# Order of VectorE and SyncE work around the attention steps of a four-layer kernel

## The chip, the cores and the metric

The kernel runs on one core of a Trainium2 chip. TensorE (PE) multiplies matrices, VectorE (DVE), ScalarE (ACT) and GpSimd (POOL) compute beside it, SyncE (SP) issues most of the transfers, and GpSimd issues the gathers. The metric is the time of one execution on the device in microseconds. The kernel before has a median of 1561.31 us in 4 runs (1559.86 to 1563.71).

## The reference

An input x of 8 sequences, 128 tokens each and 512 features, all in 32-bit floats, goes through four layers of the form x + ffn(cond(x)):

```
x = x + L0_ffn(L0_cond(x))   # gated MLP with adapters; two experts of 8
x = x + L1_ffn(L1_cond(x))   # low-rank adapters chosen by sequence; 8 weighted experts
x = x + L2_ffn(L2_cond(x))   # attention over cached and new keys; linear layer with a routed low-rank part
x = x + L3_ffn(L3_cond(x))   # linear layer, two of 8 experts; 16 of 64 rank-8 experts
```

The change lies in the third layer's attention. It has 32 query heads and 8 key heads of width 128. The queries and keys of the 128 new tokens are normalised (root mean square), scaled and rotated by position. Each sequence attends to 512 cached tokens, gathered through a table of pages, of which those behind the sequence's length are masked, and to its own 128 new tokens:

```
scores = einsum('bqhd,bkhd->bhqk', q, k_all) * SCALE
probs = softmax(where(valid, scores, -1e30))
o = einsum('bhqk,bkhd->bqhd', probs, v_all)
out = einsum('bse,de->bsd', o.reshape(b, s, 4096), Wo)
```

## The kernel before, in words

All of it is one program with x held on chip. Attention takes 32 steps, n = 0 to 31: eight key heads (`qd`), and for each of them four pairs of sequences (`p`). A key head serves four query heads, so a step treats two sequences j = 0, 1 with four heads each. The steps are software-pipelined; the body of the loop in `run` (L1271) does, in this order:

- `weigh(n, 0)` (L1118): five score matmuls of sequence 0 (`st`, keys by queries, four chunks `kT` of cached keys and one `kTn` of new keys), each followed by ScalarE's exponential into `pT`.
- `added(n, 0)` (L1140): four VectorE sums over the chunks, into `part`: chunks 0 and 1, chunks 2 and 3, the two together, chunk 4. It is a generator, so a step can be taken out of it and the rest later.
- `divided(n - 1)` (L1183): the output of the step before times the inverse sums `R`, into `oT`; `outputs(n - 1)` (L1189): four VectorE sums (`os`) of blocks of `oT`.
- `project(n + 1)` (L996): queries, keys and values of the next step. The product is done by a scheme with seven block products in place of eight (`seven`, L948), with sums of input blocks (`xs` by `tokens`, weight `factors`) made by VectorE beforehand. `rotate` (L1037) then makes the crossed terms of the rotation on GpSimd (`vq`, `vk`) and the straight terms on VectorE; that of the keys is handed back as a function, `keys_terms`.
- `leave(n - 1)` (L1197): the product with Wo, again by `seven` (`wo_one`, `wo_two`, `wo_six`), added to `y`. At named places in it `seven` calls hooks, and these decide where VectorE's other work stands.
- `fetch(n + 1)` (L1109), `gather`: reading of the turned queries and keys, gathers of values.
- `weigh(n, 1)` mixed with `mix(n, 0)` (`av`, L1172), `added(n, 1)`, `summed(n)` (L1149, sum over keys by matmuls with ones, `sum`), `inverted(n)` (L1160, the reciprocal, copied four times by VectorE and spread over partitions by three SP transfers `R<-R`), `mix(n, 1)`, then the cached keys and token sums of step n + 2.

Queries and keys are turned by a VectorE transpose of 32 by 32 blocks into a tile `qkt` or `kt`. Both are the same one buffer. SP writes the tile to device memory in four transfers (`turned_new`, `turned_cached`) and reads it back in another layout (`qT`, `kTn`, `kT`). So the next transpose into that buffer waits until the writes before it have landed.

In `seven` the hook "u2" stands right after VectorE's two sums `u`. Then come two matmuls into the bank `six`, VectorE's addition of that bank into y (`c22`), and the hook "c22". The bank's last matmuls multiply by the fourth weight factor, and they write the bank that VectorE has to read first:

```
into(p5, s1, t1, fresh)
kept(dve.tensor_tensor(u[:, 1], p6, u[:, 0], ALU.add))
now("u1")
kept(dve.tensor_tensor(u[:, 2], p5, u[:, 1], ALU.add))
now("u2")
into(six, s3, t3, True)
c22(six, u[:, 2])
now("c22")
into(one, a12, b21, False)
...
into(six, a22, t4, False)
```

The Wo weights of a key head are loaded behind its first pair; of their four factors (`o_s`) one to three are made in `project` of the following step, and the last one in `leave` of that step, so in steps 1, 5, 9 and so on to 29. Step 0 has no output of a step before it, and step 31 no next one to project; for both, `run` has branches of their own.

What is wrapped in `kept` stays in the program's order on its engine. What is not, is placed by the scheduler that builds the program. The two weight loads of the fourth part of the kernel, `load_w2` and `load_aw` (L1742, L1746, 1 MB each, called in step 30), and the addition of a bias to x on GpSimd (`shifted`, L1779) are not wrapped. The profile shows them where the scheduler put them: the loads in step 30, the two halves of the bias in steps 28 and 30.

After step 31 follow the linear layer of layer three and layer four.

Of the kernel before, what the change touches and what calls it, by code (L numbers as in the profile page):

```python
# [783 lines left out]
def attention(tc, a, x, ident, lens, kvrow, part, ww, wop, ypool, sums, rot, eps, psa, c2, chunks, mm):  # L784
# [7 lines left out]
    pe, act, dve, pool, sp = nc.tensor, nc.scalar, nc.vector, nc.gpsimd, nc.sync  # L792
# [52 lines left out]
    W, WO = {}, {}  # L845
# [45 lines left out]
    def every(ops):  # L891
        for _ in ops:
            pass
# [34 lines left out]
    def tokens(n, tag="xs"):  # L928


        qd, p = steps[n]
        b = 2 * p
        if 0 < qd < NQ - 1 and p in kept_sums:
            S[n]["A"] = kept_sums[p]
            return iter(())
        parts = [x[:, 2 * h : 2 * h + 2, (b + j) * P : (b + j + 1) * P] for j in range(2) for h in range(2)]
        if 0 < qd < NQ - 1:
            if not kept_sums:
                late.append(late[0].tile([P, NP, 4, 2, P], F32, tag="yT", name="xs_all"))
            S[n]["A"], ops = combine(late[1][:, p], *parts)  # L940
            kept_sums[p] = S[n]["A"]
        else:
            S[n]["A"], ops = combine(
                wk.tile([P, 4, 2, P], F32, tag=tag, name=f"xs_{n}", **({"bufs": 1} if tag == "xs" else {})), *parts
            )
        return ops
# [118 lines left out]
    def rotated(n):  # L1065
        for m in "qk":
            r, u = S[n]["r" + m]
            kept(dve.tensor_tensor(r, r, u, ALU.add))
# [6 lines left out]
    def normed(n):  # L1075

        s = S[n]
        r, rs = s["rq"][0], s["rs"]
        kept(dve.reciprocal(rs, rs))
        kept(dve.tensor_tensor(r, r, rs[:, :, 0:REP].unsqueeze(3).to_broadcast([P, 2, REP, HD]), ALU.mult))  # L1080

    def turn_cached(n):

        s = S[n]
        t = wk.tile([P, 4, 8, 32], F32, tag="kt", name=f"kt_{n}", bufs=1)
        for j in range(2):
            kept(dve.transpose(
                t[:, :, 4 * j : 4 * j + 4, :], s["kc"][j].rearrange("p c (b d) -> p b c d", b=4)
            ))
        s["kT"] = wk.tile([P, 4, 8, 32], F32, tag="kT", name=f"kT_{n}")  # L1090
        written(turned[n], t)
        return lambda: kept(sp.dma_start(s["kT"], turned[n].rearrange("b i a m d -> (b i) a m d")))
# [5 lines left out]
    def turn(n, by=(sp,)):  # L1098

        s = S[n]  # L1100
        m = 2 * REP
        t = wk.tile([P, 4, m + 2, 32], F32, tag="kt", name=f"qkt_{n}", bufs=1)
        done = kept(dve.transpose(t, s["both"].rearrange("p m (b d) -> p b m d", b=4)))
        s["qT"] = wk.tile([P, 4, m, 32], F32, tag="qT", name=f"qT_{n}", bufs=1)
        s["kn"] = wk.tile([P, 2, 4, 32], F32, tag="kTn", name=f"kTn_{n}", bufs=1)
        written(turned_new[n], t, by)
        return done

    def fetch(n, between=lambda: None):  # L1109
        s = S[n]  # L1110
        m = 2 * REP
        src = turned_new[n].rearrange("b i a m d -> (b i) a m d")
        kept(sp.dma_start(s["qT"], src[:, :, 0:m, :]))
        between()
        for j in range(2):
            kept(sp.dma_start(s["kn"][:, j], src[:, :, m + j, :]))
# [72 lines left out]
    def outputs(n):  # L1189
        oT = S[n]["oT"]  # L1190
        S[n]["oA"], ops = combine(
            late[0].tile([P, 4, 2, P], F32, tag="os", name=f"os_{n}"),
            *(oT[:, j, 2 * h : 2 * h + 2, :] for j in range(2) for h in range(2)),
        )
        return ops
# [75 lines left out]
    def run(pool_, end_of, bank, keep):  # L1271
        late.append(pool_)
        y2 = ypool.tile([P, NB, D], F32, tag="y", name="y2")
        Y.append(y2)
        pool.memset(y2, 0.0)

        idle = psa.tile([P, 512], F32, tag="mm", name="idle_q", bufs=3)
        for _ in range(3):
            kept(pe.matmul(idle, x[:, 0, 0:P], x[:, 0, 0:512], start=True, stop=True))
        for j in range(2):  # L1280
            squares(1, "q", j, range(REP))
            squares(1, "k", j, (0,))
        rotate(1)()
        gather(1, "v")
        roots(1)
        rotated(1)
        normed(1)
        turn(1)
        end, prepared = None, iter(())
        w_ops, wo_ops = iter(()), WO[0].factors()  # L1290

        def some(ops, k=1):
            return lambda: [next(ops, None) for _ in range(k)]

        for n, (qd, p) in enumerate(steps):

            after = n + 1 if 0 < n < len(steps) - 1 else None
            weigh(n, 0)
            sums_of, outs = added(n, 0), iter(())
            next(sums_of)  # L1300
            some(w_ops)()
            if n:
                divided(n - 1)
                outs = outputs(n - 1)
            every(sums_of)
            if after:
                project(after, {
                    "u2": lambda: (every(outs), every(w_ops), some(wo_ops)()),
                    "c22": lambda: (turn_cached(2)() if n == 1 else None, some(wo_ops, 2)()),
                    "c11": lambda: (squares(after, "k", 0, (0,)), squares(after, "q", 0, (0, 1))),  # L1310
                    "c12": lambda: squares(after, "q", 0, (2, 3)),
                })
                keys_terms = rotate(after)
                if n + 2 < len(steps):
                    if steps[n + 2][1] == 0:
                        weights(steps[n + 2][0])
                    gather(n + 2, "k")
                leave(n - 1, {
                    "one": lambda: (
                        squares(after, "q", 1, range(REP)), squares(after, "k", 1, (0,)), roots(after),  # L1320
                    ),
                    "u2": lambda: (keys_terms(), every(wo_ops)),
                    "c22": lambda: (rotated(after), normed(after), turn(after)),
                })
                fetch(after)
                gather(after, "v")
            elif n:
                every(outs)
                leave(n - 1)
            else:  # L1330
                read_cached = turn_cached(1)
                every(tokens(2))
                gather(2, "k")
            if n + 2 == len(steps):
                end.load_w2()
                end.load_aw()
                end.shifted()
            mixed = mix(n, 0)
            weigh(n, 1, {2: (some(mixed),), 3: (some(mixed),), 4: (some(mixed, NC),)})
            if n == 0:  # L1340
                fetch(1, read_cached)
            every(added(n, 1))
            if 0 < n < len(steps) - 2 and steps[n + 2][1] == 0:
                w_ops = W[steps[n + 2][0]].factors()
                some(w_ops, 2)()
            summed(n)
            inverted(n)
            if n == 5:
                prepared = end.prepare(bank, lambda shape, name: wk.tile(shape, F32, tag="xs", name=name, bufs=1))
            next(prepared, None)  # L1350
            every(mix(n, 1))
            next(prepared, None)
            if n and p == 0:
                out_weights(qd)
                wo_ops = WO[qd].factors()
            if 0 < n < len(steps) - 2:
                turn_cached(n + 2)()
                every(tokens(n + 2))
            if n == 3:
                kept(keep())  # L1360
            if n == 4:
                end = end_of(kept)

            if qd == NQ - 1 and p:
                for j in range(2):
                    end.turn(y2, 2 * (p - 1) + j, bank)
            if n + 2 == len(steps):
                end.low(0, bank)
                end.anchors(0, bank)
        divided(n)  # L1370
        every(outputs(n))
        end.product(0, "st", bank)
        leave(n)
        return y2, end

    return SimpleNamespace(begin=begin, first=first, run=run, scratch=scratch)


# [307 lines left out]
def ending(tc, a, out, x, ident, bias3, experts, early, tile_of_w2, tile_of_aw, chunks, mm, kept=lambda i: i):  # L1686
# [4 lines left out]
    pe, act, dve, pool, sp = nc.tensor, nc.scalar, nc.vector, nc.gpsimd, nc.sync  # L1691
# [48 lines left out]
    W = {}  # L1740

    def load_w2():  # L1742
        W["2"] = tile_of_w2([P, DC, D], "WT2")
        sp.dma_start(W["2"], chunks(a["W2T"]))

    def load_aw():  # L1746
        W["a"] = tile_of_aw([P, DC, D], "AwT")
        sp.dma_start(W["a"], chunks(a["AwT"]))

    def turn(y2, b, bank):  # L1750
        if not Y2T:
# [387 lines left out]
```

## Time and profile before

| | us |
|---|---|
| median of 4 runs | 1561.31 |
| range of the runs | 1559.86 to 1563.71 |
| the profiled execution | 1558.25 |
| its span, first to last instruction | 1556.4 |
| TensorE busy in the span | 1521.5 |
| VectorE busy | 1023.6 |
| GpSimd busy | 828.8 |
| layers one and two, up to the first steps of attention | 330 |
| attention, steps 0 to 31 (330.61 to about 1402) | 1072 |
| the rest of layer three | 32 |
| layer four | 122 |

How to read what follows. A row of the timeline has the start in us from the span's start, the length, the engine, the line of the kernel, the operation, out<-in by the program's names, the shape and the count; in brackets stands the idle time of the engine ahead of it and what ended that. A 32-bit matmul instruction of the program shows as two, so `x4` are two of them. An instruction's listed length includes the time in which its result drains, so rows of one engine can overlap. The table of waits gives for each pair of waiting and releasing line the total in us, how often, and the longest. In the table by stretches, PEclk is the share of TensorE's clock that was granted. "Landing" is the time at which a transfer's last completion is recorded.

### The profile page before, as it was taken

The numbers are of one execution on the slowest core, as the hardware profiler recorded it, in microseconds if no ns is written. First come the engines' busy times: TensorE is split into PE (matmuls) and PEld (weight loads), VectorE is DVE, ScalarE is ACT, GpSimd is POOL, SyncE is SP. The second block draws the span as 40 slices with busy tenths as digits, with TensorE's granted clock in tenths as the row PEclk, the third lists the DMA queues.
The fourth block names the chain that finished last, engine by engine and source line by source line (L and its number), as shares of the span: only waits on it lengthen the run. The fifth ranks groups of instructions, "written<-read, shape, count | busy, mean of one in ns | idle before, by whom it ended". The sixth has DMA issues, their size and how long they took to land.

```text
span 1556.4 us, 18566 instructions
## 1 busy us (share of the span) xinstructions
PE 1521.5 (98%) x5991; PEld 930.3 (60%) x5991; DVE 1023.6 (66%) x1963; ACT 538.3 (35%) x1324; POOL 828.8 (53%) x842
## 2 busy tenths in 40 slices
PE   9999999989999999999999999999999999999998
PEld 7888886435555555556555556555555555568743
DVE  4665334477878777777877778777777878743141
ACT  1111110143445443445444445444445434321110
POOL 1341105285767777767777667777667777600000
PEclk9999999999999999999999999999999999999899
DMA  9111002143654444553454444455444435530000
GB/s 301 43 42 31 1 0 65 48 131 106 173 157 141 143 123 126 151 156 99 132 164 131 140 121 136 113 147 169 131 126 141 121 102 152 150 87 12 0 21 36
DMA packets 156682, 169.89 MB, mean 109 GB/s; under 512 B 54144, under 2 KB 127040, under 8 KB 156448
## 3 DMA queue, kind: packets, MB, share of 16 engines
q1 hardware_dynamic: 138144, 131.27, 29.7%
q0 software_dynamic: 17056, 36.49, 7.8%
q10 hardware_dynamic: 1376, 0.85, 0.2%
q8 instruction: 50, 0.82, 0.2%
q14 instruction: 56, 0.46, 0.1%
HBM read 113.89 MB, written 42.07 MB: 100 GB/s over the span
## 4 chain that ended last, share of the span: by engine, by line
PE 89%; DVE 5%; DMA 2%; POOL 1%; issue 1%; ACT 1%; SPq 0%; DVEq 0%; ACTq 0%; POOLq 0%
PE av L1177 17%; PE st L1126 16%; PE g L362 8%; PE q_six L962 7%; PE q_one L962 5%; PE q_five L962 5%; PE wo_two L962 5%; PE dn L362 5%; PE wo_six L962 3%; PE wo_one L962 3%; PE eo_l L53 3%; PE z L53 2%; PE h L1704 2%; PE o L53 2%; PE midp_l L53 1%; PE sum L1155 1%
## 5 line engine op out<-in xcount | busy, mean ns | idle before, releaser
L905 POOL DMA_INDIRECT kn<-in_k_cache,kvrow_k x256 | 281.4, 1099 | 73.3 <-issue 66.0
L1177 PE MATMUL av<-pT,vals 128*128 128x512 f32 x640 | 300.1, 599 | 0.0
L905 POOL DMA_INDIRECT vals<-in_v_cache,kvrow_v x256 | 260.3, 1017 | 73.4 <-issue 42.5
L1130 ACT ACTIVATE pT<-st,hide 128x512 f32<-128x512 f32 x256 | 176.0, 688 | 328.1 <-PE st L1126 328.1
L1126 PE MATMUL st<-qT,kT 128*128 128x512 f32 x512 | 235.8, 593 | 3.0 <-DMA qT<-turned_new 3.0
L1051 POOL TENSOR_TENSOR vq<-q,txq 128x256 f32<-128x256 f32 x128 | 118.3, 954 | 172.6 <-ACT sqq L1035 116.9
L1177 PEld LDWEIGHTS av<-pT,vals 128*128 128x128 f32 x640 | 119.5, 191 | 144.9 <-issue 142.8
L1126 PEld LDWEIGHTS st<-qT,kT 128*128 128x128 f32 x512 | 96.9, 190 | 111.5 <-issue 106.7
L1146 DVE TENSOR_TENSOR part<-pT 128x512 f32<-128x512 f32 x128 | 88.4, 693 | 79.2 <-ACT pT L1130 79.0
L962 PE MATMUL q_one<-q,x 128*128 128x384 f32 x256 | 93.0, 486 | 0.0
L1035 ACT ACTIVATE sqq<-q 128x128 f32<-128x128 f32 x256 | 79.4, 310 | 11.6 <-DVE q L1011 4.9
L1162 DVE RECIPROCAL rr<-sum 128x256 f32<-128x256 f32 x32 | 56.2, 1756 | 41.2 <-PE sum L1155 41.2
L962 PEld LDWEIGHTS q_one<-q,x 128*128 128x128 f32 x256 | 48.5, 190 | 39.8 <-issue 14.3
L962 PE MATMUL q_six<-q_s,xs_all 128*128 128x384 f32 x192 | 69.8, 486 | 0.0
L962 PE MATMUL wo_one<-o,oT 128*128 128x256 f32 x256 | 65.7, 379 | 0.0
L1126 PE MATMUL st<-qT,kTn 128*128 128x512 f32 x128 | 65.4, 592 | 0.0
L1215 POOL TENSOR_TENSOR y<-y,uo 128x512 f32<-128x512 f32 x32 | 41.3, 1291 | 43.5 <-DVE y L1207 43.0
L1016 ACT COPY q<-q_one 128x256 f32<-128x256 f32 x32 | 11.9, 372 | 148.7 <-PE q_one L962 148.7
L962 PE MATMUL wo_two<-o_s,os 128*128 128x256 f32 x256 | 60.6, 380 | 2.6 <-DVE os L921 2.4
L1130 ACT ACTIVATE pT<-st,rs 128x512 f32<-128x512 f32 x64 | 44.0, 687 | 38.4 <-PE st L1126 38.4
L962 PEld LDWEIGHTS wo_one<-o,oT 128*128 128x128 f32 x256 | 48.5, 190 | 13.5 <-PE st L1126 0.6
L429 POOL TENSOR_TENSOR ws<-wu 128x256 f32<-128x256 f32 (+1 forms) x9 | 6.4, 714 | 91.5 <-DMA wu<-in_WuT 91.5
(396 smaller groups left out, 2744.0 us busy)
## 6 DMA issues: line engine op xcount, KB each, us to landing
turned_new<-qkt SPq DMA_DIRECT2D x126, 160.0 KB
turned_cached<-kt SPq DMA_DIRECT2D x128, 128.0 KB
kT<-turned_cached SPq DMA_DIRECT2D x32, 512.0 KB
qT<-turned_new SPq DMA_DIRECT2D x32, 512.0 KB
R<-R SPq DMA_DIRECT2D x96, 128.0 KB
q<-in_WqT SPq DMA_DIRECT2D x8, 1024.0 KB
o<-in_WoT SPq DMA_DIRECT2D x8, 1024.0 KB
kn<-in_k_cache,kvrow_k POOLq DMA_INDIRECT x256, 3.0
```

The source lines that it names most:

```text
L53: pe.matmul(o, lhsT, rhs, start=start, stop=stop)
L362: pe.matmul(o, lhsT, rhs, start=start, stop=stop, skip_group_check=True)
L905: kept(pool.indirect_dma_start(out=d[:, c, :], out_offset=None, in_=kc if what == "k" else vc, in_offset=bass.IndirectOffsetOnAxis(ap=kvro ...
L962: kept(pe.matmul(o, l[:, c, :], r[:, c, :], start=start and c == 0, stop=c == 1, skip_group_check=True))
L1035: kept(act.activation(sq, S[n][m][:, j, i, :], AF.Square, accum_out=S[n]["ssq"][:, j, col : col + 1]))
L1051: kept(pool.tensor_tensor(to, t[:, b, :, hi : hi + 64], wx[:, b, lo : lo + 64].unsqueeze(2).to_broadcast(list(to.shape)), ALU.mult,))
L1126: kept(pe.matmul(ps, s["kT"][:, c, 4 * j : 4 * j + 4, :] if c < 4 else s["kn"][:, j], s["qT"][:, :, REP * j : REP * (j + 1), :].rearrange( ...
L1130: kept(act.activation(pT[:, c, :, :].rearrange("p i t -> p (i t)"), ps, AF.Exp, **(dict(bias=hide[:, b, c : c + 1]) if c < 4 else dict(bia ...
L1146: kept(dve.tensor_tensor(o, l, r, ALU.add))
L1162: kept(dve.reciprocal(r, S[n]["sum"]))
L1177: kept(pe.matmul(ps, v[:, c, :], pT[:, c, :, :].rearrange("p i t -> p (i t)"), start=c == 0, stop=c == NC - 1, skip_group_check=True,))
L1215: kept(pool.tensor_tensor(t, t, u.unsqueeze(1).to_broadcast([P, 2, HW]), ALU.add))
```

## The change

It has three parts.

First, in the steps 1 to 30 the hook "u2" of `leave` is gone. The keys' straight term and the remaining weight factor move into the hook "c22", so VectorE does the addition of the bank `six` into y first, then the factor, then the keys' straight term, then what stood there before.

Second, the first and the last step. In step 31 the four `os` sums of step 30 stand ahead of the last three part sums of step 31, not behind them. In step 0 the transposes of the cached keys of step 1 stand between the second and the third part sum of sequence 1, the token sums of step 2 behind the reciprocal and its copies; before, both stood ahead of all part sums of sequence 1. The reads of step 1 still follow the writes of the turned cached keys on SP's queue.

Third, the loads of W2T and AwT are kept in the program's order. They come behind the reads `qT` and `kTn` of step 31 on SP's queue and ahead of the three `R` copies of step 30. Before, W2T stood ahead of the read `kT` of step 31, AwT behind it, and one `R` copy ahead of `qT` and `kTn`, two behind them.

The matmuls and the instructions of GpSimd keep their order.

```diff
             if n:
                 divided(n - 1)
                 outs = outputs(n - 1)
+                if not after:
+                    every(outs)
             every(sums_of)
...
-                    "u2": lambda: (keys_terms(), every(wo_ops)),
-                    "c22": lambda: (rotated(after), normed(after), turn(after)),
+                    "c22": lambda: (every(wo_ops), keys_terms(), rotated(after), normed(after), turn(after)),
                 })
                 fetch(after)
                 gather(after, "v")
             elif n:
-                every(outs)
                 leave(n - 1)
-            else:
-                read_cached = turn_cached(1)
-                every(tokens(2))
-                gather(2, "k")
...
             weigh(n, 1, {2: (some(mixed),), 3: (some(mixed),), 4: (some(mixed, NC),)})
+            sums_of = added(n, 1)
             if n == 0:
-                fetch(1, read_cached)
-            every(added(n, 1))
+                some(sums_of, 2)()
+                fetch(1, turn_cached(1))
+                gather(2, "k")
+            every(sums_of)
...
             summed(n)
             inverted(n)
+            if n == 0:
+                every(tokens(2))
...
     def load_w2():
         W["2"] = tile_of_w2([P, DC, D], "WT2")
-        sp.dma_start(W["2"], chunks(a["W2T"]))
+        kept(sp.dma_start(W["2"], chunks(a["W2T"])))
 
     def load_aw():
         W["a"] = tile_of_aw([P, DC, D], "AwT")
-        sp.dma_start(W["a"], chunks(a["AwT"]))
+        kept(sp.dma_start(W["a"], chunks(a["AwT"])))
```

## Prediction

> **What bounds the kernel now.** I read the page first: the busy table and the chain.
>
> ```profile
> PE 1521.5 (98%) x5991; PEld 930.3 (60%) x5991; DVE 1023.6 (66%) x1963; ACT 538.3 (35%) x1324; POOL 828.8 (53%) x842
> ...
> PE 89%; DVE 5%; DMA 2%; POOL 1%; issue 1%; ACT 1%; SPq 0%; DVEq 0%; ACTq 0%; POOLq 0%
> ```
>
> TensorE is the bound, so a reordering of other engines is worth only the TensorE waits that it removes. The view of TensorE's waits ranks them (total us, times, longest):
>
> ```profile
> PE sum L1155 <- DVE part L1146: 4.7, 2, 3.4
> PE wo_six L962 <- DVE y L1207: 3.7, 9, 0.8
> PE st L1126 <- DMA qT<-turned_new: 3.0, 2, 1.8
> PE wo_two L962 <- DVE os L921: 2.4, 1, 2.4
> ```
>
> The change aims at the first, second and fourth, 10.8 us in all. The timeline gives their places: the sums in steps 0 and 30, wo_six in steps 1, 5, 9, 13, 17, 21, 25, 29 (small ones fall below the view's limit), 28 and 30, wo_two in step 31. From score to score an undisturbed step takes 33.01 us.
>
> I count a matmul's delay from starts, since ends are modelled: a pass takes 0.43 us at 512 columns, 0.322 at 384, 0.216 at 256, and each instruction makes two.
>
> **A. Steps 1 to 30: the y sum ahead of the keys' term.** TensorE and VectorE in step 5:
>
> ```profile
> 503.05 1.03 PE L962 MATMUL wo_six<-o_s,os 128*128 128x256 f32 x4
> ...
> 504.78 1.03 PE L962 MATMUL wo_two<-o,os 128*128 128x256 f32 x4
> 506.08 1.13 PE L962 MATMUL wo_six<-o_s,oT 128*128 128x256 f32 x4 [0.27 <-DVE y L1207]
> ```
>
> ```profile
> 503.78 0.42 DVE L977 TENSOR_TENSOR uo<-wo_two,uo 128x256 f32<-128x256 f32 x1
> 504.12 0.70 DVE L1056 TENSOR_TENSOR r<-k,tsk 128x256 f32<-128x256 f32 x1
> 504.75 0.94 DVE L869 TENSOR_TENSOR o_s<-o,o_s 128x512 f32<-128x512 f32 x1
> 505.61 0.41 DVE L1207 TENSOR_TENSOR y<-wo_six,y 128x256 f32<-128x256 f32 x1
> ```
>
> The last wo_six could start at 504.78 + 4 x 0.216 = 505.64. It starts at 506.08, 0.44 late, because y has to read its bank first and stands behind the keys' term and a weight factor. By the same count the eight steps that have such a factor lose 0.71 (step 1), 5 x 0.44 (5, 9, 13, 21, 25), 0.32 (17) and 0.14 (29): 3.4 us.
>
> After: y, factor, keys' term. The added wait is y's, for the first half of wo_six, and behind it on VectorE stand the factor, the keys' term, the rotation and the turn that feeds qT. Step 31 has no keys' term, so the trace already shows y right behind the two u sums:
>
> ```profile
> 1372.23 0.43 DVE L977 TENSOR_TENSOR uo<-wo_two,uo 128x256 f32<-128x256 f32 x1
> 1372.57 0.42 DVE L1207 TENSOR_TENSOR y<-wo_six,y 128x256 f32<-128x256 f32 x1
> ```
>
> There wo_six starts at 1371.50 and the second u 0.73 later, as in step 5 (503.05 and 503.78), and y follows without a gap. So the wait costs nothing: y takes 504.12 to 504.53, and the factor, which the last wo_six also needs, ends near 504.45 + 0.94 = 505.39, with 0.25 to spare. VectorE's total up to the turn stays the same. The cover is gone only if y waits over 0.25 us. What is late next is qT: by the trace's landing records it lands 0.80 us ahead of step 2, and 0.72 to 2.63 ahead of the steps behind the later factors, so it holds by 0.1 (step 2) and 0.28 (step 26) at the least. I take **-3.3**. Bounds: -3.4, and 0 if qT takes all of it.
>
> In the other steps y is not late today and nothing is gained. Steps 28 and 30 are the exception: the keys' term takes 2.08 us there, beside a 4.58 us addition on GpSimd, and wo_six is 0.95 late. Without that, TensorE reaches the sum 0.95 earlier. But part, which waits through the rotation for GpSimd's vq (until 1272.24 and 1341.92), ends only 0.11 and 0.06 us before the sum's second half now, against 1.30 in other steps. The stall moves to the sum: **0**. Bounds: 0 and -1.9.
>
> **B. Step 31: added outputs ahead of the sum of part.** wo_two starts at 1369.70, its floor is 1366.23 (wo_one) + 0.86 + 0.04 = 1367.13. Now oT (to 1366.64), three part sums, then os. After, os follows oT, its second sum ends near 1367.45 instead of 1369.55, and wo_two starts near 1367.55: -2.15. The part sums then end near 1370.3, u and y near 1371.5, and the last wo_six needs y at 1371.9: covered by 0.4.
>
> R, without which oT can't start, has changed neighbours on SP's queue. Now W2T and AwT go out at 1333.78 and 1335.07, and this step's qT stands behind one of three R copies, which hold it to 1356.59. After, the order is qT, kTn, W2T, AwT, three R copies. qT can go at about 1351.4 (its writes land at 1351.34). That is worth nothing: qT lands at 1361.79, just when TensorE is free anyway (1361.84), so earlier data finds TensorE busy. The loads go out near 1353.5 and R keeps its issue at 1355.85, but 2 MB stand ahead of it. R lands at 1365.16 now, oT starts at 1365.35. The two loads with kT between took 9.9 us from first issue to last landing; from 1353.5 that is 1363.4, and the R copies need about 2 more: 1365.6, so oT is 0.3 later and **-1.8** is left. Bounds: R at 1363.9 (-2.15), or at the rate of a WoT load (8.35 us for one megabyte at 1289.37), near 1371.5 (+4.1). I take the rows of the same two loads.
>
> **C. Step 0.** The sum waits until 347.49:
>
> ```profile
> 341.97 1.30 DVE L1087 STREAM_TRANSPOSE kt<-kn 128x512 f32<-128x512 f32 x2 [2.47 <-DMA turned_new<-qkt]
> ...
> 347.49 0.66 PE L1155 MATMUL sum<-part,ones 128*32 128x128 f32 x8 [3.42 <-DVE part L1146]
> 348.08 5.89 PE L1177 MATMUL av<-pT,vals 128*128 128x512 f32 x10
> 353.80 3.60 PE L1126 MATMUL st<-qT,kT 128*128 128x512 f32 x8
> ```
>
> After, two part sums (1.3 us) fill VectorE's idle 2.47 us, their inputs being there by 340.15; the token sums (1.5 us) go behind the reciprocal, where 5.26 us are idle. The last part then ends near 344.7, and av, ten passes, near 349.3: 4.5 us earlier. But the transposes still wait for the buffer until 341.97, so SP still writes the cached keys at 343.30, asks for kT at 347.57, and kT lands at 352.92. GpSimd's gather waits for the transposes as before, and R goes out 2 us earlier, behind kTn. So the next score starts near 353.0: -0.8, and TensorE is idle for 349.4 to 353.0 instead. That idle time has a price of its own. The table by stretches:
>
> ```profile
> core 0: us, PE busy (x), PEclk, DMA share, GB/s
> 343.97:347.38 3.41, 0.10 (x4) 1.00 0.78 190
> 347.38:350.79 3.41, 3.30 (x11) 0.50 0.88 304
> ```
>
> Behind 3.4 idle us the granted clock was 0.50 for 3.41 us. The new idle stretch, 3.5 us, is as long; by that row it is followed by 3.41 us at half clock, 1.7 us lost: **+0.9** net. Bounds: -2.7 (full clock, and kT landing in the 3.5 us that it takes in other steps), +1.9 (R's packets hold kT by 1 us more).
>
> The Trainium skill, "TensorE: Matmul & The Clock Gate", section "What's actually happening", says that the clock falls to half after at least one idle window of about 3.4 us, and that windows run freely. The 3.41 us in the row agree; read strictly, an idle 3.5 us holds a whole window in few phases, and the sum below would be 5.9 instead of 4.2. The row at 1443.05, half clock behind a window in which TensorE was listed 2.92 us busy, says that a window need not be wholly idle.
>
> **Sum.** -3.3 + 0 - 1.8 + 0.9 = -4.2 us. The profiled execution took 1558.25 us (span 1556.4), which would become 1554.05. It lies 3.06 us under the median of the runs, 1561.31; I take the difference over: **1557.1**. About 0.2%, 3.1 us, is what a measurement of this kernel can tell from no change.
>
> **Rivals.**
> - No half clock in step 0: +0.9 becomes -0.8, so 5.9 us less, **1555.4**. For it: windows in which about 60% is idle are not always followed by half clock (1369.70, 1.67 busy of 3.41, stayed at 1.00). Against it: the row above. 0.25.
> - The step's end as in A, but new half clock or a later R takes a part back: step 30's stall at the sum grows from 1.5 to 2.5 us, and a half-clock window there costs 1.7; R 2 us late costs as much. About 2.3 us less, **1559.0**. 0.22.
> - qT takes the place of A (slack of only 0.72 to 1.0 at most of these steps): 0.9 us less, **1560.4**. Against it: VectorE's work up to the turn is the same. 0.06.
> - Slower: R behind 2 MB at the WoT rate, landing at 1371.5. wo_two then starts near 1373.8, 4.1 late instead of 1.8 early, with half clock behind the idle time (1.7): -3.3 + 0.9 + 4.1 + 1.7 = +3.4, **1564.7**. It decides against the change from R at about 1370. The Trainium skill, "DMA: Bandwidth & Descriptors", section "Queues, rings and completion order", says that descriptors of a ring are consumed in ring order; by it R waits for all of both loads. For the rival: the row at 1289.37, with gathers beside it as here. Against it: these loads' own rows. 0.07.
>
> **How the numbers follow.** Forecast 0.40, rivals 0.25, 0.22, 0.06, 0.07. Faster by over 0.2%: 0.40 + 0.25 and a little of the second rival, 0.67; within: 0.26; slower: 0.07. The range reaches from the first rival, less 1.6 for a half-clock window that the runs of before may have behind step 31's stall, to the third: 1553.8 to 1560.5.
>
> **What would show it.** A: no wait of wo_six for y in steps 1 to 25, steps of 33.0 instead of 33.55 us; wrong if st waits for qT in steps 2, 6, 10 and so on. Steps 28 and 30: the waits now at the sum. B: wo_two near 0.4 behind its floor, and R's landing beside oT. C: the sum's second half near 344.7, then a wait of st for kT near 353, and the granted clock behind it. The forecast is wrong if y's wait shows on VectorE in each step, if R lands after 1367 on this scale, or if kT comes much earlier.

## The result and the profile after

The changed kernel takes 1558.11 us (median of 32 runs, 1552.26 to 1562.74), the kernel before 1560.6 us (52 runs on the same chips, 1557.0 to 1565.02). The ratio is 0.9981, 95% interval 0.9974 to 0.9988: 2.5 us less by the medians. Forecast were 4.2 us less, 1557.1. One of the six runs of a_only below took 2643.71 us at a granted clock of 0.565 and is left out of its ratio.

The profiled execution of the changed kernel took 1560.51 us (span 1558.6), 2.4 above its median; that of before lay 3.1 below the median of the four runs beside it, 2.4 below that of the 52. So the two executions must not be subtracted as a whole: I subtract them stage by stage. First the page of the changed kernel, busy table and chain:

```profile
PE 1523.3 (98%) x5991; PEld 934.6 (60%) x5991; DVE 1014.0 (65%) x1963; ACT 538.1 (35%) x1324; POOL 824.4 (53%) x842
...
PE 88%; DMA 4%; DVE 3%; POOL 2%; ACT 1%; issue 1%; SPq 0%; ACTq 0%; DVEq 0%
```

TensorE is still the bound, but in the chain VectorE has given two per cent (5 to 3) and DMA has taken them (2 to 4). TensorE's waits say the same with names:

```profile
PE st L1126 <- DMA qT<-turned_new: 4.4, 4, 1.9
PE st L1126 <- DMA kT<-turned_cached: 4.3, 1, 4.3
PE sum L1155 <- DVE part L1146: 3.6, 3, 2.3
PE wo_one L962 <- DVE oT L1187: 2.7, 1, 2.7
```

wo_six no longer waits for y, and wo_two no longer for os. In their place st waits for kT (step 1), wo_one for oT (step 31), and st two times more for qT. The table below has the length of each stretch, from start to start of TensorE's instructions, in us, for the two kernels (the changed one in two profiled executions on different chips) and for two kernels told of below.

| stretch | before | changed | changed, 2nd | ab_late | best |
|---|---|---|---|---|---|
| span's start to st of step 0 | 330.61 | 332.16 | 330.44 | 331.20 | 331.42 |
| to the second st of step 1 (C, and A in step 1) | 43.85 | 44.79 | 42.45 | 43.22 | 39.00 |
| to the second st of step 27 (A) | 863.78 | 861.88 | 861.01 | 860.86 | 861.16 |
| to st of step 31 (steps 28 to 30) | 123.60 | 123.30 | 125.07 | 124.88 | 124.06 |
| to the second st of step 31 (B, loads) | 13.11 | 14.99 | 16.26 | 11.01 | 11.01 |
| to TensorE's last instruction | 175.42 | 175.37 | 176.82 | 175.39 | 175.40 |

("Second st" is the score that follows the output projection within a step.) The 1.55 us of the first row lie in code that the change doesn't touch: that execution had a half-clock window (a stretch with a granted clock of 0.50) at 27.86, in layer one, and TensorE is 1.6 us later behind it.

**A.** Step 5 of the changed kernel, TensorE and then VectorE:

```profile
506.24 1.03 PE L962 MATMUL wo_six<-o_s,os 128*128 128x256 f32 x4
...
508.83 1.03 PE L962 MATMUL wo_six<-o_s,oT 128*128 128x256 f32 x4
```

```profile
506.96 0.42 DVE L977 TENSOR_TENSOR uo<-wo_two,uo 128x256 f32<-128x256 f32 x1
507.31 0.42 DVE L1207 TENSOR_TENSOR y<-wo_six,y 128x256 f32<-128x256 f32 x1
507.64 0.68 DVE L869 TENSOR_TENSOR o_s<-o,o_s 128x512 f32<-128x512 f32 x1
508.24 0.68 DVE L1056 TENSOR_TENSOR r<-k,tsk 128x256 f32<-128x256 f32 x1
```

y follows the second u without a gap, and the last wo_six has no bracket: the step is at its floor, 2.59 us from one wo_six to the other where it was 3.03. The weight factor takes 0.68 instead of 0.94.

**C.** Step 0 and the start of step 1:

```profile
346.13 0.43 PE L1155 MATMUL sum<-part,ones 128*32 128x128 f32 x8 [0.51 <-DVE part L1146]
346.49 4.56 PE L1177 MATMUL av<-pT,vals 128*128 128x512 f32 x10
355.34 5.37 PE L1126 MATMUL st<-qT,kT 128*128 128x512 f32 x8 [4.30 <-DMA kT<-turned_cached]
```

The sum's wait fell from 3.42 to 0.51, and st now waits 4.30 for the cached keys: the wait has changed its place.

**B and the loads.** VectorE and TensorE in step 31:

```profile
1368.50 1.29 DVE L1187 TENSOR_TENSOR oT<-av,R 128x512 f32<-128x512 f32 x2 [2.95 <-DMA R<-R]
```

```profile
1369.33 2.05 PE L962 MATMUL wo_one<-o,oT 128*128 128x256 f32 x4 [2.66 <-DVE oT L1187]
```

SP's queue in that step (its rows are issues; the landing records are in the text):

```profile
1351.77 0.58 SPq L1113 DMA_DIRECT2D qT<-turned_new  x1
...
1353.74 0.62 SPq L1745 DMA_DIRECT2D WT<-in_W2T  x1
1354.40 0.59 SPq L1749 DMA_DIRECT2D AwT<-in_AwT  x1
1356.19 2.35 SPq L1167 DMA_DIRECT2D R<-R  x3
```

W2T landed at 1362.05, AwT at 1367.84, R at 1368.37: 12.2 us after its first issue, where R in the steps before takes 4 to 5 (R of step 26: 1218.34 to 1222.93). The half-clock window that follows (1369.29 to 1372.70) is seen in wo_one's listed length, 2.05 instead of 1.03.

### The profile page after: what moved, and what is told of

Read it like the earlier page. It is cut to its first block, busy times and chain, and to the rows that moved or that the text cites. A ratio compares the mean times of both kernels' runs of the same rounds, so it can differ in the third digit from the quotient of the medians.

```text
span 1558.6 us, 18563 instructions
## 1 busy us (share of the span) xinstructions
PE 1523.3 (98%) x5991; PEld 934.6 (60%) x5991; DVE 1014.0 (65%) x1963; ACT 538.1 (35%) x1324; POOL 824.4 (53%) x842
## 4 chain that ended last, share of the span: by engine, by line
PE 88%; DMA 4%; DVE 3%; POOL 2%; ACT 1%; issue 1%; SPq 0%; ACTq 0%; DVEq 0%
PE st L1126 16%; PE av L1177 16%; PE g L362 8%; PE q_six L962 7%; PE q_one L962 5%; PE wo_two L962 5%; PE q_five L962 5%; PE dn L362 5%; PE wo_one L962 3%; PE wo_six L962 3%; PE eo_l L53 2%; PE z L53 2%; PE h L1705 2%; PE o L53 2%; PE midp_l L53 1%; PE sum L1155 1%
## 5 line engine op out<-in xcount | busy, mean ns | idle before, releaser
L905 POOL DMA_INDIRECT kn<-in_k_cache,kvrow_k x256 | 273.5, 1068 | 73.3 <-issue 68.2
L362 PE MATMUL g<-xs,ws 128*128 128x256 f32 (+1 forms) x240 | 55.4, 381 | 0.0
```

The source lines that it names most:

```text
L362: pe.matmul(o, lhsT, rhs, start=start, stop=stop, skip_group_check=True)
L905: kept(pool.indirect_dma_start(out=d[:, c, :], out_offset=None, in_=kc if what == "k" else vc, in_offset=bass.IndirectOffsetOnAxis(ap=kvro ...
```

## The experiments

Two kinds of chip came up. In the runs of the result and on the second chip of the experiments the kernel before takes 1560 to 1561 us, on three others 1580 to 1581; what differs is told at the end. A run is compared only with the kernel before on its own chip.

**The parts, one at a time** (first chip, before: 1580.6 us). a_only is the diff's two lines at "u2" and "c22" alone. b_only:

```diff
+                if not after:
+                    every(outs)
...
-                every(outs)
```

w_only is `kept(...)` around the two loads alone, c_only the remaining lines (step 0).

> The y sum ahead of the factor and the keys' term in steps 1 to 30, nothing else. Theory (this part carries the gain): 2.4 to 3.4 us less than before, no wait of wo_six for y in steps 1 to 29 but 28, and the 0.95 us of steps 28 and 30 found again as a longer wait at the sum. Rival (qT's transfer takes the wait over): under 1 us less, and st waits for qT in steps 2, 6, 10, 14, 18, 22 and 26 for about what wo_six waited.

Measured: 0.9962 (0.9948 to 0.9976), 6.0 us less by the ratio, 7.7 by the medians. All waits of wo_six for y are gone, and st is 0.2 to 0.7 us late for qT in five of the seven steps that the rival names (2, 10, 18, 22, 26). The direction and the mechanism hold; the size is about twice what the wo_six waits give, on a chip where VectorE runs later against TensorE than in the profile of before. Part of the surplus shows beside the three runs below, which lack this edit: there q_five waits for VectorE's sum `uq` (4.5, 2.5 and 1.8 us in b_only, w_only and c_only), in a_only it doesn't, and from the second st of step 1 to that of step 27 they take 3 to 7 us longer (879.16, 876.44 and 880.18 for 873.39).

> The added outputs ahead of the part sums in step 31, with the two weight loads where the scheduler had them, nothing else. Theory: R lands as before, 0.2 us ahead of oT, so wo_two starts 2.1 us earlier and the median is 1.5 to 2.2 us lower. Rival (the order alone is worth nothing, because something else is late in step 31): no change within 0.5 us.

Measured: 0.9988 (0.9977 to 1.0), 1.9 us less by the ratio, 3.3 by the medians; no wait of wo_two for os in step 31. The interval reaches to no change; that the new order pays by itself rests on the trace, and on ab_late below.

> The two weight loads kept in the program's order, ahead of the R copies of step 30, nothing else. Theory (R queues behind 2 MB): R lands 2 to 4 us later than before, oT with it, and wo_one and wo_two wait; 1 to 4 us slower. Rival (the loads are hidden either way): no change within 0.5 us, R landing at the time of before.

Measured: 1.001 (0.9992 to 1.0027), unclear in time, but not in the trace: R issued at 1372.44 lands at 1384.73, 12.3 us later; wo_one waits 1.24 for oT, wo_two another 2.41 for os, and the stretch from st to the second st of step 31 takes 17.50 us, with half clock from 1388.39 on (14.61 and 16.01 in a_only and c_only, where the loads stand as before).

> The order of step 0 alone. Theory (the wait moves from the sum to the cached keys' transfer, and half clock follows): the sum's wait falls from 3.4 to about 0.5 us, st of step 1 waits about 3.5 to 4.3 us for kT, half clock behind it, and the median is 0.5 to 1.7 us higher. Rival (the shorter wait at the sum is a gain): 0.8 to 2.7 us lower.

Measured: 1.0009 (0.9989 to 1.0028), unclear. The trace has the forecast's sequence: the second half of the sum 0.65 late, st of step 1 held after av, half clock behind it.

```profile
346.30 0.42 PE L1155 MATMUL sum<-part,ones 128*32 128x128 f32 x8 [0.65 <-DVE part L1146]
...
354.93 6.28 PE L1126 MATMUL st<-qT,kT 128*128 128x512 f32 x8 [3.72 <-issue]
```

(Many records of landings are missing on this chip, and the wait is listed under "issue": kT's last record is at 353.76, 1.2 us ahead of st, qT of step 1 has none. What ended the wait here is not shown.) Eight passes of st take 6.28 instead of 3.60. So the gain is in A and B; what W (the loads) and C give back shows in the traces and not clear of noise in the times. By the ratios the four add up to -5.0 us there, by the medians to -7.7.

**The loads behind R, and the half clock** (second chip, before: 1561.09 us).

> The changed kernel itself, as the common mark for the other three runs. On the chip of the first result it was 2.5 us faster than the kernel before; the four parts run alone on another chip add up to -6.0 - 1.9 + 1.5 + 1.4 = -5.0 us. If the parts add, this run is 2 to 6 us faster than the kernel before. It shows again R of step 30 landing some 12 us after its issue, a wait of wo_one for oT of 1.4 to 2.8 us in step 31, and a wait of st for kT of some 4 us in step 1 with a half-clock window behind it.

Measured: 0.999 (0.9979 to 1.0002), 1.8 us less by the medians, a little under the 2 to 6 expected. R lands 14.0 us after its issue, wo_one waits 3.26 us, a half-clock window follows: 16.26 us for the stretch of step 31. But behind step 1's wait for kT, 3.58 us, there is **no** half clock this time. The table by stretches, laid on the grid on which this execution's half-clock windows begin (they all begin at one phase of 3.413 us, as at 1347.83 and 1368.31):

```profile
core 0: us, PE busy (x), PEclk, DMA share, GB/s
347.71:351.13 3.42, 1.69 (x4) 1.00 0.99 315
351.13:354.54 3.41, 1.56 (x4) 1.00 1.04 238
354.54:357.95 3.41, 3.41 (x9) 1.00 0.15 43
```

and the same stretch in the first profile of the changed kernel, on its own grid:

```profile
348.70:352.11 3.41, 2.35 (x6) 1.00 0.98 243
352.11:355.53 3.42, 0.19 (x1) 1.00 1.05 272
355.53:358.94 3.41, 3.41 (x5) 0.50 0.35 93
```

In one the grid cuts the wait into halves, and each window is 0.46 to 0.49 busy; in the other a window lies wholly inside it, 0.06 busy. So a like wait (listed 3.58 and 4.30 us) is followed by 3.41 us of half clock or by none, by where it falls: it costs some 1.7 us more or nothing.

ab_late has A and B, step 0 as before, and the loads kept, but behind the R copies:

```diff
-                end.load_w2()
-                end.load_aw()
                 end.shifted()
...
             inverted(n)
+            if n + 2 == len(steps):
+                end.load_w2()
+                end.load_aw()
```

> The first two parts of the change alone (the order at a step's end, and the added outputs of step 31 ahead of the part sums), step 0 as before, and the two weight loads behind the three R copies of step 30 instead of ahead of them. Theory (B pays by itself, and what the changed kernel loses in step 31 is R standing behind 2 MB): R of step 30 lands 4 to 5 us after its issue, at most 0.3 us of wait of wo_one or wo_two in step 31, and the time is 3 us under the changed kernel's (1.5 for the loads, 1.4 for step 0). Rival (the outputs' order costs what it saves, R late or not): step 31 as long as in the changed kernel, and only step 0's 1.4 us gained. Second rival (the loads, now later, delay the closing part): the loads land over 10 us later and a wait for WT or AwT stands in the closing part.

Measured: 1554.07 us, 0.9954 (0.994 to 0.9967), 7.0 us under before and 5.2 under the changed kernel on the same chip, where 3 were expected. By the table above, step 31's stretch alone is 5.25 us shorter than in the changed kernel beside it:

```profile
1364.54 1.03 PE L962 MATMUL wo_one<-o,oT 128*128 128x256 f32 x4
1365.84 1.97 PE L962 MATMUL wo_two<-o_s,os 128*128 128x256 f32 x8 [0.28 <-DVE os L921]
```

wo_one doesn't wait, and wo_two comes 0.40 behind its floor (wo_one's start and 0.90), as forecast. R lands 3.9 us after its issue (1352.52 to 1356.39). The loads land at 1360.71 and 1365.15 and nobody waits for them.

best is ab_late with, in step 0, the cached keys of step 1 turned ahead of that step's new ones, and the token sums of step 2 behind the reciprocal as in the changed kernel:

```diff
         rotate(1)()
+        read_cached = turn_cached(1)
         gather(1, "v")
...
-            else:
-                read_cached = turn_cached(1)
-                every(tokens(2))
-                gather(2, "k")
+            else:
+                gather(2, "k")
...
             inverted(n)
+            if n == 0:
+                every(tokens(2))
```

> The kernel of the run before this one, and in step 0 the cached keys of step 1 turned ahead of that step's new ones, so that their transposes no longer wait for the buffer of the new ones behind step 0's scores, and kT goes out earlier. Theory (in step 0 both the sum's wait of 3.4 us and its half clock, 1.7 us, come from transposes that wait for that buffer): the sum of sequence 1 within 0.6 us of its floor, kT there before st of step 1 needs it, no half-clock window in steps 0 and 1, from st of step 0 to st of step 1 about 18.5 instead of 23.2 us, and 4 to 5 us under the run before. Rival (qT of step 1 then comes late in place of kT, or qT of step 2 binds behind it): a wait of st for qT of 2 us or more, and less than 2.5 us gained.

Measured: 1550.09 us, 0.9928 (0.9913 to 0.9942), 11.0 us under before, 4.0 under ab_late: the fastest kernel of the study. The sum is at its floor, and st of step 1 waits half a microsecond:

```profile
344.46 1.00 PE L1155 MATMUL sum<-part,ones 128*32 128x128 f32 x16
345.39 4.56 PE L1177 MATMUL av<-pT,vals 128*128 128x512 f32 x10
350.50 1.96 PE L1126 MATMUL st<-qT,kT 128*128 128x512 f32 x4 [0.55 <-DMA kT<-turned_cached]
```

From st of step 0 to st of step 1 it takes 19.08 us instead of 23.19, and no half-clock window follows. The changed kernel moves the token sums too but leaves the transposes waiting for the buffer; so the wait that is left there, of st of step 1 for kT, came from the buffer. How much of the old wait at the sum the token sums alone were was not run.

after_warm adds matmuls on the tokens, into a bank that nobody reads, behind step 0's last av:

```diff
             every(mix(n, 1))
+            if n == 0:
+                idle = psa.tile([P, 512], F32, tag="mm", name="idle_k", bufs=3)
+                for _ in range(14):
+                    kept(pe.matmul(idle, x[:, 0, 0:P], x[:, 0, 0:512], start=True, stop=True))
```

> The changed kernel with 14 matmuls of 512 columns on the tokens, into a bank that nobody reads, behind the last av of step 0: they fill some 3.0 of the about 4 us in which st of step 1 waits for kT. Theory (the half clock behind that wait costs time of its own): no window of 0.50 behind kT, and the scores, queries and outputs of step 1 start 1.7 us earlier against st of step 1, so 1.7 us faster than the changed kernel. Rival (the half clock is covered, because qT of step 2 binds by then): the window goes and the time stays, within 0.4 us. Second rival (the matmuls delay kT or st themselves): slower by up to 3 us, with no wait of st left in step 1.

Measured: 1561.8 us, 1.0004 (0.9994 to 1.0014). My count was wrong by four: I had taken a matmul for one pass of 0.21 us, and it is two of 0.43, so 14 of them took from 348.61 to 360.62, 12.0 us, and held st back themselves. No half clock followed, so the second rival's delay came, 2.5 us over the changed kernel; the run doesn't tell the other two apart.

**Once more on other chips** (before: 1579.69 us for the next three, 1580.86 for the last).

> The changed kernel, with one thing undone: the two weight loads stand behind the three R copies of step 30, not ahead of them. Theory (W is what the changed kernel loses, about 2.3 us in R and 1.7 in the half clock behind the wait): from st of step 31 to its second half 11.0 us as in the run with A and B (15.0 and 16.3 in the two profiles of the changed kernel), R landing 4 to 5 us after its issue, and the kernel about 6 us under the kernel before: 1.4 above the run with A and B, which has step 0 as before. Rival (the loss lies in the loads' own packets beside R, not in their place in the queue): R lands late again, and 3 us or less under the kernel before.

Measured: 1571.75 us, 0.9953 (0.9935 to 0.9971), 7.9 us under before by the medians. R lands 3.9 us after its issue by the few landing records that this trace has, and wo_one doesn't wait. The stretch of step 31 takes 12.47 us, with a half-clock window of other origin in it (1372.93 to 1376.34, behind step 30); without its 1.5 us, 11.0.

> The run with matmuls in step 1's wait again, with the number put right: a matmul is two passes of 0.43 us, so 14 of them took 12.0 us and held st of step 1 back by some 7.6. Now 3 of them, 2.6 us, which end before kT lands; TensorE stays idle for 1 to 1.7 us. Theory (a half clock behind this wait costs 1.7 us, wherever the wait falls on the grid of 3.41 us windows): no window of 0.50 in step 1, st of step 1 not later, and 0.5 to 1.7 us under the changed kernel, since one of its two profiles had no such window. Rival (the half clock is covered by qT of step 2): the same time as the changed kernel within 0.4 us, with a wait of st for qT of 0.5 us or more in step 2.

Measured: 1569.8 us, 0.9932 (0.991 to 0.9953), the same as the changed kernel beside it, not 0.5 to 1.7 us less. A half-clock window stands in step 1 all the same (359.93), behind a wait of st for ScalarE that only this kind of chip shows (2.03 us). Inconclusive.

> The changed kernel once more, as the mark for the two runs beside it on the same chip. Expected, from its other two comparisons (2.5 and 1.8 us under the kernel before): 1.5 to 3 us under. In step 31 a wait of wo_one of 2.5 us or more, with a half-clock window behind it; in step 1 a wait of st for kT of about 4 us, with a half-clock window behind it or not, by where it falls on the grid of windows.

Measured: 1569.23 us, 0.9941 (0.992 to 0.9961): 10 us less than before on this chip, not 1.5 to 3. R lands 12.1 us after its issue, wo_one waits 1.47 and not 2.5, a half-clock window follows, 14.45 us for the stretch; st of step 1 waits 3.0 for kT, with no half clock behind it. On this chip after_late is 2.5 us slower than the changed kernel by the medians, though its step 31 is 2.0 us shorter: the single runs of each spread over 9 us, and the time doesn't show what the loads' place costs.

> The changed kernel with the two weight loads behind the R copies, once more, since on the chip of its first run the times of one kernel spread over 10 us and releases from TensorE to VectorE came late, so that 2 us could not be told. Theory (the place of the loads costs the changed kernel 2.3 us in R and often 1.7 in half clock): on a chip where the kernel before takes 1560 to 1562 us, 5 to 6.5 us under it, where the changed kernel was 2.5 and 1.8 under; 11.0 us from st of step 31 to its second half. Rival (what the loads' place costs in step 31 is given back elsewhere): 1.5 to 3.5 us under it, as the changed kernel, with R in time.

Measured: 1573.84 us, 0.9942 (0.9922 to 0.9963), on a chip of the slower kind again. In the trace wo_one doesn't wait for oT, and step 31's stretch takes 12.46 us, again with a half-clock window in it (from 1377.16). The expectation named a chip of 1560 to 1562 us, which this is not; the cost of the loads' place in time rests on ab_late beside the changed kernel, where step 0 differs too.

## Why the prediction was right in its sign and too large

**A, forecast -3.3: the mechanism right, the size near because misses cancel.** The table's second and third rows hold it. Step 1 by itself gives 0.63 (ab_late, which has step 0 as before: 43.85 to 43.22); forecast were 0.71. From there to step 27 the forecast is -2.45 (3.3 less step 1 and step 29's 0.14); measured are -1.9, -2.8, -2.9 and -2.6. From second st to second st, step by step, the waits for y gave 3.1 there and not 2.5: 0.50 to 0.56 in steps 5, 9, 13, 21 and 25, where 0.44 were counted, and 0.43 in step 17 for 0.32. Step 18 gave 0.4 to 0.8 that the forecast doesn't have: in before, q_six waits there for VectorE's copy of the values (`vals`, listed 0.4), in the other four not. Then qT took back 0.7 to 1.8, the forecast's rival in small: its slack was to hold by 0.28 in step 26 and by 0.1 in step 2, and st is late for it in step 26 in all four profiles (0.99, 0.30, 0.74 and 0.66) and in step 2 in three (0.59, 0.21 and 0.42, and 0.01 in ab_late). In step 26 the turn ends 10.27 us before TensorE would be free for st in before and 10.0 in the other four, so VectorE is 0.3 later. The rest is the transfer: qT takes 4.32 us from issue to landing in before, 5.66 in the first profile, 4.7 to 5.3 in the others. Why it does stays open.

**Steps 28 and 30, forecast 0: right, with the second rival beside it.** The wait moved from wo_six to the sum. In step 30, before and then changed:

```profile
1352.32 0.43 PE L1155 MATMUL sum<-part,ones 128*32 128x128 f32 x8 [1.24 <-DVE part L1146]
```

```profile
1352.66 0.43 PE L1155 MATMUL sum<-part,ones 128*32 128x128 f32 x8 [2.29 <-DVE part L1146]
```

The stretch changes by -0.3. In the second profile and in ab_late a half-clock window stands behind that stall (1347.83, 1349.52), and the stretch is 1.5 and 1.3 longer. That is the rival's 1.7, by phase.

**C, forecast +0.9 with half clock and -0.8 without: both came.** Compared with ab_late's 43.22 the changed kernel has 44.79 (+1.6, half clock) and 42.45 (-0.8, none). The +1.6 exceeds +0.9 because kT took 6.4 us from issue to landing, not 5.35. The forecast and the first rival were one mechanism: the phase of the windows decides which comes.

The Trainium skill, "TensorE: Matmul & The Clock Gate", section "What's actually happening", has windows of some 3.4 us that run freely. The traces agree: within each of the fourteen executions profiled, every half-clock window begins at the same phase of 3.413 us, within 0.05 us, and the phase differs between executions. A window needn't be idle throughout: in steps 0, 1, 30 and 31 of the fourteen, all 17 windows at full clock with TensorE listed busy 0.41 or less were followed by half clock. Of the 32 from 0.42 to 0.69 four were (0.46, 0.57, 0.62 and 0.67), and so were two of 0.83, all six on chips where the kernel before takes 1580 us. So the strict reading that the prediction weighed is not borne out here. (The row that the first rival leans on, 1.67 busy of 3.41, is 51% idle, not about 60%.)

**B, forecast -1.8: the step that failed**, because of the loads. The order itself gives 2.1 (13.11 to 11.01 in ab_late and best). The failed step is R's landing: "1365.6, so oT is 0.3 later". R landed at 1368.37, past the 1367 that the forecast had named as a sign of being wrong, and oT started at 1368.50, against st of step 31 2.9 us later than before (6.37 for 3.51), and behind TensorE's wait came a half-clock window. So B and the loads together made +1.9 in the first profile, and +3.2 in the second, in place of -1.8. The second rival names what came, a later R and a half-clock window, with R 2 us late; the slower rival's premise, that R waits for both loads, held too, at a part of its price. What I mis-sized is one term: the pair of loads took 9.9 us in the trace of before, and I added it to 1353.5. Here it took 14.1 us (1353.74 to 1367.84). The view of the transfers from the pair's first issue to its last landing, before and then changed:

```profile
DMA packets 1201, 2.63 MB, mean 266 GB/s; under 512 B 48, under 2 KB 48, under 8 KB 1200
```

```profile
DMA packets 2955, 3.60 MB, mean 255 GB/s; under 512 B 1280, under 2 KB 1705, under 8 KB 2954
q1 hardware_dynamic: 2698, 3.06, 71.3%
q0 software_dynamic: 256, 0.52, 14.7%
```

In before the pair moved with kT alone. Here qT and kTn were asked for 2 us ahead of it, three R copies behind it, and beside it run the gathers of step 31's values by GpSimd (0.52 MB, the last row). At the rate of before 3.60 MB would take 13.5 us, so the bytes would explain nearly all of the 14.1; no run took the gathers or qT away to show it. The forecast counted R's copies apart, as 2 us, and left out the rest, though its slower rival speaks of gathers. Behind R, in ab_late and best, the pair takes 10.3 and 10.4 us with 2.52 MB in the span. From qT's issue to the last landing the lot takes 16.6 and 18.8 us in the two profiles of the changed kernel, 17.0 and 17.2 in ab_late and best: the order gains or loses nothing there that shows beyond this scatter, it decides who is last. By the Trainium skill, "DMA: Bandwidth & Descriptors", section "Queues, rings and completion order", the descriptors of a ring are consumed in ring order; the landings agree, R 0.53 us behind AwT.

**The sum.** From st of step 0 to the second st of step 31 before takes 1044.34 us by the table, the changed kernel 1044.96 and 1044.79, ab_late 1039.97, best 1035.23. Against the forecast of -4.2 the first profile is 4.8 too long: 3.7 in step 31, 0.7 in C, 0.6 in A, -0.3 in steps 28 to 30; the second has 5.0 in step 31 and 1.5 in steps 28 to 30, less 1.7 in C and 0.2 in A (step 29's 0.14 is the small rest of both). So in the traces the changed kernel is 0.5 to 0.6 us longer over these steps, while the medians fell by 2.5. That the time came near the forecast is in part luck, since B's miss is met by something that no term of the sum holds. By its number the outcome lies nearest the second rival, 2.3 us less. What the traces miss seems to lie in before, whose profiled execution is a short one, and the only one. All four kernels stand better by their medians than by this table, by 3.1, 2.3, 2.6 and 1.9 us, about the 3.1 by which that execution lay below the median of its four runs (2.4 below that of the 52). The forecast carried these 3.1 us over to the changed kernel, whose profiled executions lie above their medians (2.4 and 1.2). What else before loses in its other executions no profile shows.

## What to carry to other kernels

A transfer that TensorE waits for is not to stand behind a bulk load on its queue, though the load's issue hides in idle time: count all the bytes that go beside the load, on every queue, gathers included, and not the load alone. A wait that is removed in front of a fixed arrival (kT, R, qT) comes back at that arrival: look first at what makes it arrive late, here a shared buffer, whose release was worth more than the whole change. An idle time of TensorE near 3.4 us had two prices here, 1.7 us or nothing; forecast it with both.

## What the runs showed of the hardware

On the three chips on which the kernel takes 1580 us, nearly all instructions have the same lengths (of 78 groups of instructions between 400 and 1200 us, 77 agree within 1.1% in after_third and after_again), but the releases from TensorE to VectorE are recorded later. On the second chip, step 4, the first sum of a query follows the matmuls that it reads at once (row of the timeline):

```profile
493.03 0.56 DVE L975 TENSOR_TENSOR uq<-q_six,uq 128x384 f32<-128x384 f32 x1 [0.37 <-PE q_six L962]
```

The same kernel in the same step on one of the three (after_third):

```profile
498.17 0.56 DVE L975 TENSOR_TENSOR uq<-q_six,uq 128x384 f32<-128x384 f32 x1 [1.70 <-PE q_five L962]
```

There q_six started at 494.71 and q_five at 496.00, so the sum could start near 496.3; its release is recorded at 498.07, and q_five's 0.06 behind it. From step 2 on, the median delay between the listed end of those matmuls and the sum is 0.11 us in each of six profiles of the one kind of chip, and 1.0 to 1.6 in eight of the other. q_six then waits for VectorE (in after_third 7.1 us in 13 steps). The chips differ by 20 us for one program, and the same edit was worth 2 us on one kind and 10 on another (0.999 and 0.9941). What holds the release back, and why A gains more there beyond the waits named above, stays open.
